# Layer 2: the first row's norm for the mixer, made and turned inside the FFN's steps of the second row

## The chip, the cores and the metric

The kernel runs on one core of a Trainium2 chip. Its time is the device time of one execution in microseconds. Of several executions the median counts.

## The reference, cut to what matters

The network has four layers on a float32 activation `x` of 2 rows (batch) x 512 tokens x 256 features. Every layer is a half-weighted FFN, a mixer and the same FFN again, each on a norm of `x` without weights:

```
def _layernorm(x, axis=-1, eps=1e-05):
    m = jnp.mean(x, axis=axis, keepdims=True)
    v = jnp.var(x, axis=axis, keepdims=True)
    return (x - m) / jnp.sqrt(v + eps)
...
    x = x + 0.5 * _L2_ffn_ref(_layernorm(x, axis=-1), L2_ffn_wg, L2_ffn_W, L2_ffn_b)
    x = x + _L2_attn_ref(_layernorm(x, axis=-1), L2_attn_W_in, ...)
    x = x + 0.5 * _L2_ffn_ref(_layernorm(x, axis=-1), L2_ffn_wg, L2_ffn_W, L2_ffn_b)
```

Layer 2's FFN is a routed one with 8 experts of 256 x 256. A token's logits go through a softmax, the best expert is taken, and its output plus bias is weighted by its probability. Layer 2's mixer is a state-space model with 8 heads of 64, a state of 128, a causal convolution of 4 taps, and a gate. Its input product is

```
        zxbcdt = u @ W_in
        z = zxbcdt[..., :D_INNER]
        xBC = zxbcdt[..., D_INNER:D_INNER + CONV_DIM]
        dt = zxbcdt[..., D_INNER + CONV_DIM:]
        dt = jax.nn.softplus(dt + dt_bias)
```

where `u` is the normed `x`. Every token of `u` needs only its own token of `x`. The mixer works along a row, and the two rows don't meet in it.

## The kernel before, in words

`x` stays on the chip for the whole program, as 8 chunks of 128 tokens (one token a partition). Chunks 0 to 3 are the first batch row, 4 to 7 the second. TensorE (PE) multiplies over partitions, so a normed chunk (tokens on partitions) has to be turned before it is multiplied by a weight. PE does that by a product with an identity (`transpose`), and ACT or DVE copies the result out of PSUM.

**Layer 2's FFN** (`l2_ffn`) goes through the chunks in steps. The step of chunk c computes its experts, two experts a product (`experts`, product at L1622, its two additions into `x` on DVE at L1627), turns the next chunk n = c + 1 (`turn`, L1590, copy at L1592), routes it (`route`, L1600 to L1614), and adds the biases of chunk c (`bias_turn` L1633, `bias` L1642 and L1643). The statistics of later chunks (`measure`, which calls `scale`: bn_stats and aggregate on DVE at L191 and L192, two operations on POOL at L200 and L201) run ahead. `centre` (L205) makes the normed chunk. All chunks of a row are final in `x` once their own step is over.

**Layer 2's mixer** (`mamba`, with `few` true, as it has one group of 8 heads) begins with `layernorm_T`. It makes a tile `xT` for the turned norm of both rows and gives out the steps by which a row gets there: `measure` (statistics of four chunks on DVE, L215 and L216; one pair of POOL operations for all four, L224 and L225), `norm` (four L230), `turn` (four transposes into a PSUM bank at L184, a copy by `evac` at L130 or L132). `row(0)` does all of these for row 0 at once. Then `decay_sums(0)` multiplies the row by the dt columns (`pd`, L1762) and goes on to softplus and the decays (L1765 to L1816); `conv_b` and `conv_c` multiply by the B and C columns (`pp`, L1823), scale on ACT (L1826), and add three taps on DVE (L1830). Row 1's statistics, norm and turns are placed among these steps. The decays are written to HBM and read back by DMA (L1801, L1924, L1927), and then the chunks of the row are worked on.

`warm` (L164) multiplies constants by constants into a PSUM tile that nobody reads. In front of the mixer `few` gives 4 of them.

**What sets the order.** The program is written as one stream; a planner then orders each engine's instructions by their dependencies and its own estimates of durations. `in_order` pins the order as written: in the FFN for PE alone, in the mixer's opening for PE, ACT and DVE, and in its steps for POOL too. What is not pinned, as DVE, ACT and POOL in the FFN, may be moved ahead or back. Engines run their instructions strictly in that order. A PSUM pool that opens on banks of a closed one waits for the closed one's last readers. `f2m`, the FFN's PSUM pool, has all 8 banks; the mixer's `psM` has 3 in rotation. The weights are fetched early: `wb` (B, C and dt columns) far ahead and `wx` (`fetch_wx`, L1876) on SP's queue before the FFN begins.

Layer 2's FFN is built twice, before and after the mixer; layer 3 follows with its own FFN and a larger mixer of the same function.

Of the kernel before, what the change touches and what calls it, by code (L numbers as in the profile page):

```python
# [10 lines left out]
F32 = mybir.dt.float32  # L11
# [7 lines left out]
P = 128  # L19
B, S, D = 2, 512, 256  # L20
T = B * S
NC = T // P
CB = S // P
KD = D // P
# [59 lines left out]
class Net:  # L84
# [143 lines left out]
    def layernorm(self, pool, xn, b, mv, rstd):  # L228
# [8 lines left out]
            )  # L237
        return xn

    def layernorm_T(self, es, psum):  # L240


        xT = es.enter_context(self.tc.tile_pool(name="xT", bufs=1)).tile([P, KD, T], F32, name="xT")
        p = es.enter_context(self.tc.tile_pool(name="ln", bufs=1))

        made = {}

        def measure(b):
            made[b] = self.scales(p, b)

        def norm(b):
            made[b] = self.layernorm(p, p.tile([P, CB, D], F32, tag="xn", name="xn"), b, *made[b])

        def turn(b, k):
            self.transpose_tokens(made[b], xT, psum, b, k)

        def row(b):
            if b in self.pending:
                by_chunks(b)
                return  # L260
            measure(b)
            norm(b)
            for k in range(KD):
                turn(b, k)

        def by_chunks(b):

            xn = p.tile([P, CB, D], F32, tag="xn", name="xn")
            ps = [psum.tile([P, S], F32, tag="mm", name="ps_tr") for _ in range(KD)]
            ms = {}  # L270
            for cc in range(CB + 1):
                if cc < CB:
                    self.settle(b, cc + 1)
                    ms[cc] = self.scale(p, b * CB + cc, b * CB + cc)
                if cc > 0:
                    j = cc - 1
                    self.centre(xn[:, j, :], b * CB + j, *ms[j])
                    if j < CB - 1:
                        self.warm(psum, 1)
                    for k in range(KD):  # L280
                        self.nc.tensor.transpose(
                            ps[k][:, j * P : (j + 1) * P], xn[:, j, k * P : (k + 1) * P], self.ident
                        )
            for k in range(KD):
                self.evac(xT[:, k, b * S : (b + 1) * S], ps[k])

        return xT, row, measure, norm, turn

    def rms(self, pool, out, h, w):
# [1249 lines left out]
    @contextmanager  # L1539
    def l2_weights(self):  # L1540

        nc, tc, a = self.nc, self.tc, self.a
        E = 8
        pre = "L2_ffn_"
        with tc.tile_pool(name="f2keep", bufs=1) as keep:
            self.w8T = keep.tile([P, KD, E, D], F32, name="w8T")
            self.b8 = keep.tile([E, D], F32, name="b8")
            self.wg8 = keep.tile([P, KD, E], F32, name="wg8")
            nc.sync.dma_start(self.wg8, a[pre + "wg"].rearrange("(k p) e -> p k e", p=P))
            nc.sync.dma_start(self.b8, a[pre + "b"])  # L1550
            with tc.tile_pool(name="f2pm", bufs=4, space=PSUM) as psM:
                for e0 in range(0, E, 4):
                    wn = self.w("w8")[:, : 4 * KD * D].rearrange("p (e c d) -> p e c d", e=4, c=KD)
                    for e in range(4):
                        nc.sync.dma_start(wn[:, e], a[pre + "W"][e0 + e].rearrange("(c p) d -> p c d", p=P))
                    for k in range(KD):
                        for e2 in range(0, 4, 2):
                            ps = psM.tile([P, 2, KD, P], F32, tag="mm", name="ps_w8")
                            for e in range(2):
                                for c in range(KD):  # L1560
                                    nc.tensor.transpose(
                                        ps[:, e, c, :], wn[:, e2 + e, c, k * P : (k + 1) * P], self.ident
                                    )
                            self.evac(
                                self.w8T[:, k, e0 + e2 : e0 + e2 + 2, :].rearrange("p e d -> p (e d)"),
                                ps.rearrange("p e c d -> p (e c d)"),
                            )
            yield

    def l2_ffn(self):  # L1570


        nc, tc = self.nc, self.tc
        E = 8
        with ExitStack() as es:
            sb = es.enter_context(tc.tile_pool(name="f2", bufs=3))
            st = es.enter_context(tc.tile_pool(name="f2s", bufs=1))
            psM = es.enter_context(tc.tile_pool(name="f2m", bufs=8, space=PSUM))
            ms, xts, ws, wTs = {}, {}, {}, {}

            def measure(c):
                ms[c] = self.scale(st, c, c)
# [54 lines left out]
            def bias(c):  # L1637
                if c < 0:
                    return
                xc = self.x[:, c, :]  # L1640
                pb = psM.tile([P, D], F32, tag="mm", name="pb")
                nc.tensor.matmul(pb, wTs[c], self.b8, start=True, stop=True)  # L1642
                nc.vector.tensor_tensor(xc, xc, pb, ALU.add)  # L1643

            tail = {}
            for c in range(-1, NC):
                n = c + 1
                if n == 0:
                    measure(0)
                    measure(1)  # L1650
                if n + 1 < NC and n:
                    measure(n + 1)
                with self.in_order(tail, ("PE",)):
                    experts(c, 0)
                    turn(n)
                    bias_turn(c)
                    experts(c, 1)
                    route(n)
                    experts(c, 2)
                    bias(c)  # L1660
                    experts(c, 3)


    mix = {}
# [43 lines left out]
    def mamba(self, pre, win, wout, nh):  # L1708
# [4 lines left out]
        nc, tc, a = self.nc, self.tc, self.a  # L1713
# [7 lines left out]
        few = NG == 1  # L1721
        wname, win, wout = win, a[pre + win], a[pre + wout]
        with ExitStack() as es:
            psM = es.enter_context(tc.tile_pool(name=pre + "m", bufs=3, space=PSUM))
            xT, row, measure, norm, turn = self.layernorm_T(es, psM)
# [366 lines left out]
            later = {}  # L2092
            tail = {}
            with self.in_order(tail, ("PE", "Activation", "DVE")):
                self.warm(psM, 4 if few else 18)
                row(0)
                fetch_wx(*order[0])
                d0, d1 = decay_sums(0), decay_sums(1)
                next(d0)
                b_taps, b_silu = conv_b(0)  # L2100
                c_taps, c_silu = conv_c(0)
                next(d0)
                unit(0)
                fetch_wx(*order[1])
                x = [prep_front(us[0], 0)]
                if few:
                    measure(1)
                b_taps()
                next(d0)
                next(d0)  # L2110
                if few:
                    norm(1)
                c_taps()
                next(d0)
                x[0][0]()
                if few:
                    turn(1, 0)
                    turn(1, 1)
                else:
                    self.settle(1)  # L2120
                x.append(prep_front(us[0], 1))
                next(d0)
                next(d0)
                next(d0, None)
                x[1][0]()
                for i in range(3):
                    chunk(i)
                b_silu()
                c_silu()
                products(0)  # L2130
                x[0][1]()
                x[1][1]()
                x.append(prep_front(us[0], 2))
                prep_back(us[0], 0)
                x[2][0]()
                x[2][1]()
                prep_back(us[0], 1)
                x.append(prep_front(us[0], 3))
                exponents(ks[0])
                x[3][0]()  # L2140
                x[3][1]()
                prep_back(us[0], 2)
                exponents(ks[1])
                if few:
                    next(d1)
                raised(ks[0])
                if few:
                    next(d1)
                    next(d1)
                back = (us[0], NM - 1)  # L2150
                if few:
                    later = {0: [d1.__next__, d1.__next__, d1.__next__], 1: [d1.__next__, lambda: next(d1, None)]}
                else:
                    parts = [lambda: measure(1), None, lambda: norm(1), lambda: turn(1, 0), lambda: turn(1, 1)]
                    parts += [d1.__next__] * 7 + [lambda: next(d1, None)]
                    later = {i: [f] for i, f in enumerate(parts) if f}


            for s in range(NS):
                n, cc = steps[s]  # L2160
# [118 lines left out]
```

## Time and profile before

| | us |
|---|---|
| median of 3 runs | 1943.05 (1939.87 to 1947.71) |
| the profiled execution | 2031.53 |
| its span, first to last instruction | 2029.7 |
| layer 2's first FFN (889 to 957) | 68 |
| from there to 978, the mixer's opening up to its decays | 21 |
| rest of the mixer (978 to 1091) | 113 |
| layer 2's second FFN (to 1163) | 72 |

The profiled execution is one, and slower than those of the median, so differences are taken within it, and the sum is made against its own time. In rows of the timeline the columns are start, duration, engine, line, operation, output and inputs, shape and count. Behind them, in square brackets, stands how long the engine had been idle and who ended that.

### The profile page before, as it was taken

To read this page: it belongs to the slowest core of one execution; us is meant where nothing else is said; L and a number is where in the kernel's file an instruction comes from. 1 tells how busy PE (TensorE), PEld (TensorE's weight loads), DVE (VectorE), ACT (ScalarE), POOL (GpSimd) and SP (SyncE) were. 2 spreads that over 40 slices of the span, in tenths; PEclk is the share of its full clock that TensorE was granted. 3 is DMA by queue.
4 is the path that set the end of the run, shared out by engine and by line. 5 is a ranking of instruction groups with operands and counts; after the bars stand their busy time and mean duration, and the time that the engine had idled before them with its cause. 6 is when DMAs were issued, how large, how long until landed. Compare 5 with 4: busy or idle time off the path is not lost. (4 is left out here: it accounts for less than half of the span.)

```text
span 2029.7 us, 30414 instructions
## 1 busy us (share of the span) xinstructions
PE 1801.1 (89%) x10914; PEld 1285.4 (63%) x10914; DVE 1148.8 (57%) x2747; ACT 806.3 (40%) x1404; POOL 916.5 (45%) x915
## 2 busy tenths in 40 slices
PE   6888889999888887899788998889999899999985
PEld 4566666566666664554565466557777677777664
DVE  4522238426232357666577653478777777777633
ACT  1122215411122215420563012278777677877111
POOL 3366646530666440110033125135667456767263
PEclk8999999999998998999899998899999999999998
DMA  8145551041444360000221012344454444443132
GB/s 310 58 158 156 160 196 65 6 152 37 149 151 151 108 216 1 1 22 0 94 97 31 0 58 88 108 148 156 151 166 146 135 156 156 163 151 125 44 99 93
DMA packets 117444, 226.54 MB, mean 112 GB/s; under 512 B 22382, under 2 KB 68828, under 8 KB 117014
## 3 DMA queue, kind: packets, MB, share of 16 engines
q1 hardware_dynamic: 88134, 170.17, 25.6%
q0 software_dynamic: 20608, 48.45, 7.4%
q10 hardware_dynamic: 8528, 5.72, 0.9%
q8 instruction: 95, 1.56, 0.3%
q14 instruction: 79, 0.65, 0.1%
HBM read 195.59 MB, written 41.81 MB: 117 GB/s over the span
## 5 line engine op out<-in xcount | busy, mean ns | idle before, releaser
L538 POOL DMA_INDIRECT xe<-table,sl_get x176 | 179.9, 1022 | 230.4 <-DVE sl_get L514 145.9
L596 POOL DMA_INDIRECT rows<-ye,sl_put x176 | 176.7, 1004 | 133.6 <-DVE ye L130 43.1
L566 PE MATMUL ps_gu<-we,xeT 128*128 128x352 f32 x704 | 233.8, 475 | 0.0
L591 PE MATMUL ps_ye<-we,hT 88*128 88x256 f32 x704 | 182.2, 402 | 44.6 <-issue 23.2
L591 PEld LDWEIGHTS ps_ye<-we,hT 88*128 88x128 f32 x704 | 137.1, 198 | 90.1 <-issue 30.3
L1830 DVE SCALAR_TENSOR_TENSOR xc<-pp,L_attn_cols,xc 128x511 f32<-128x511 f32 (+2 forms) x216 | 161.4, 747 | 28.2 <-ACT xc L1826 23.0
L571 DVE SCALAR_TENSOR_TENSOR he<-se,xe,ps_gu 128x176 f32<-128x176 f32 x176 | 68.3, 396 | 192.6 <-ACT se L570 108.0
L566 PEld LDWEIGHTS ps_gu<-we,xeT 128*128 128x128 f32 x704 | 132.3, 200 | 59.5 <-issue 7.3
L1961 PE MATMUL pz<-xT,wt 128*128 128x128 f32 x1152 | 143.6, 278 | 12.3 <-ACT xt L1910 6.2
L1937 DVE SCALAR_TENSOR_TENSOR lm<-lm,jb,top 128x128 f32<-128x128 f32 x576 | 153.6, 340 | 0.0
L1961 PEld LDWEIGHTS pz<-xT,wt 128*128 128x128 f32 x1152 | 136.2, 193 | 17.6 <-issue 9.2
L2046 PE MATMUL yacc<-wt,y 128*128 128x256 f32 x576 | 143.0, 391 | 2.5 <-POOL y L2016 2.2
L1823 PE MATMUL pp<-xT,wx 128*128 128x512 f32 x288 | 140.8, 612 | 4.6 <-issue 1.2
L570 ACT ACTIVATE se<-ps_gu 128x176 f32<-128x176 f32 x176 | 54.1, 317 | 224.8 <-PE ps_gu L566 139.3
L2016 POOL TENSOR_TENSOR y<-y,sg 128x512 f32<-128x512 f32 x72 | 91.7, 1274 | 102.7 <-DVE y L2015 101.5
L1954 POOL TENSOR_TENSOR ce<-ce,CT 128x1024 f32<-128x1024 f32 x54 | 127.9, 2369 | 0.0
L1622 PE MATMUL ps_y<-w8T,xT 128*128 128x512 f32 x256 | 122.1, 611 | 0.0
L2046 PEld LDWEIGHTS yacc<-wt,y 128*128 128x128 f32 x576 | 103.8, 189 | 25.4 <-issue 10.3
L1989 PE MATMUL py<-lm,xt 128*64 128x128 f32 x1152 | 108.6, 282 | 11.9 <-DVE lm L1946 3.9
L1946 DVE TENSOR_TENSOR lm<-lm,M 128x1024 f32<-128x1024 f32 x72 | 87.1, 1215 | 48.0 <-ACT lm L1942 45.4
L164 PE MATMUL warm<-cst 128*128 128x256 f32 x348 | 97.8, 422 | 16.6 <-PEq L708 8.8
L2027 POOL TENSOR_TENSOR sqs<-sqs,sq 128x512 f32<-128x512 f32 x56 | 71.3, 1274 | 90.2 <-ACT sq L2026 90.2
(403 smaller groups left out, 3507.3 us busy)
## 6 DMA issues: line engine op xcount, KB each, us to landing
lm<-rows SPq DMA_DIRECT2D x72, 512.0 KB
ce<-rows SPq DMA_DIRECT2D x54, 512.0 KB
rows<-zero POOLq DMA_DIRECT2D x16, 768.0 KB
y<-rows SPq DMA_DIRECT2D x16, 768.0 KB
we<-in_L_ffn_w_gate_dram SPq DMA_DIRECT2D x64, 176.0 KB
we<-in_L_ffn_w_up_dram SPq DMA_DIRECT2D x64, 176.0 KB
we<-in_L_ffn_w_down_dram SPq DMA_DIRECT2D x64, 176.0 KB
we<-in_L_ffn_w_dram SPq DMA_DIRECT2D x48, 176.0 KB
```

The costliest lines, as they stand in the source:

```text
L538: nc.gpsimd.indirect_dma_start(xe[:, i, :], None, table, bass.IndirectOffsetOnAxis(get[:, e * per + j : e * per + j + 1], 0), bounds_check ...
L566: nc.tensor.matmul(pg, xeT[:, k, i * P : (i + 1) * P], wgu[:, :, k], start=(k == 0), stop=(k == KD - 1))
L591: nc.tensor.matmul(py[:, i, :], hT[:, q, i * P : (i + 1) * P], wd[:, q, :], start=(q == 0), stop=(q == 1))
L596: put_rows = nc.gpsimd.indirect_dma_start(rows, bass.IndirectOffsetOnAxis(put[:, e * per + j : e * per + j + 1], 0), y[:, i, :], None, bou ...
L1622: nc.tensor.matmul(ps, xT[:, k, :], self.w8T[:, k, 2 * e2 : 2 * e2 + 2, :], start=(k == 0), stop=(k == KD - 1))
L1823: nc.tensor.matmul(pp, wv[:, k, :], xT[:, k, b * S : (b + 1) * S], start=(k == 0), stop=(k == KD - 1))
L1830: nc.vector.scalar_tensor_tensor(out[:, 3 - w :], pp[:, : S - 3 + w], cw[:, m, w : w + 1], out[:, 3 - w :], ALU.mult, ALU.add)
L1937: nc.vector.scalar_tensor_tensor(k["lm"][:, h, :], k["lm"][:, h, :], jb[:, k["c"], n : n + 1], top, ALU.add, ALU.min)
L1954: nc.gpsimd.tensor_tensor(k["ce"], k["ce"], ct, ALU.mult)
L1961: nc.tensor.matmul(pz[:, m, :], u["wz"][:, kk, m * P : (m + 1) * P], xT[:, kk, c * P : (c + 1) * P], start=(kk == 0), stop=(kk == KD - 1),)
L1989: nc.tensor.matmul(py[i * HP : (i + 1) * HP, m, :], w[:, h * HP : (h + 1) * HP], v[:, h, :], start=(m == 0 and n == 0), stop=(n == len(src ...
L2046: nc.tensor.matmul(yacc[cc // 2][:, cc % 2, :], k["y"][:, m, :], u["wo"][:, m, :], start=(u["g"] == 0 and m == 0 and cc % 2 == 0), stop=(u ...
```

## The change

A tile `into` (named `nxT`) of the shape of the mixer's `xT` is made once, with layer 2's weights, and lives from there to the layer's end. In the first FFN of the layer (the second finds none) two functions come in. `next_measure` makes the statistics and scale of a chunk of row 0 as it is after its FFN step. `next_turn` centres it with these, turns it by two transposes into one PSUM tile, and copies it by ACT into `into`. They are written into the steps c = 3 to 6 and 4 to 7: chunk c - 4 is turned between `bias` and the last pair of experts. `layernorm_T` takes that tile as its `xT`, and `row(0)` then returns at once. In front of this mixer there are no products of constants any more; layer 3's mixer keeps its 18.

```diff
+    turned = None
     def layernorm_T(self, es, psum):
-        xT = es.enter_context(self.tc.tile_pool(name="xT", bufs=1)).tile([P, KD, T], F32, name="xT")
+        xT, self.turned = self.turned, None
+        early = xT is not None
+        if not early:
+            xT = es.enter_context(self.tc.tile_pool(name="xT", bufs=1)).tile([P, KD, T], F32, name="xT")
...
         def row(b):
+            if b == 0 and early:
+                return
...
             self.wg8 = keep.tile([P, KD, E], F32, name="wg8")
+            self.into = keep.tile([P, KD, T], F32, name="nxT")
...
-            ms, xts, ws, wTs = {}, {}, {}, {}
+            ms, xts, ws, wTs, nms = {}, {}, {}, {}, {}
+            into, self.into = self.into, None
+            self.turned = into
+
+            def next_measure(c):
+                if into is not None and 0 <= c < CB:
+                    nms[c] = self.scale(st, f"n{c}", c)
+
+            def next_turn(c):
+                if c not in nms:
+                    return
+                xn = self.centre(sb.tile([P, D], F32, tag="nxn", name="nxn"), c, *nms.pop(c))
+                pt = psM.tile([P, KD, P], F32, tag="mm", name="pt_nx")
+                for k in range(KD):
+                    nc.tensor.transpose(pt[:, k, :], xn[:, k * P : (k + 1) * P], self.ident)
+                nc.scalar.copy(into[:, :, c * P : (c + 1) * P], pt)
...
                     route(n)
                     experts(c, 2)
                     bias(c)
+                    next_turn(c - 4)
                     experts(c, 3)
+                    next_measure(c - 3)
...
             with self.in_order(tail, ("PE", "Activation", "DVE")):
-                self.warm(psM, 4 if few else 18)
+                if not few:
+                    self.warm(psM, 18)
                 row(0)
```

## The prediction

> **What bounds the kernel now.** I read three views: the page for the whole program, the busy time by stage for layer 2, and the timeline between its first FFN and its mixer. The page says that TensorE (PE) is the busiest engine.
>
> ```profile
> PE 1801.1 (89%) x10914; PEld 1285.4 (63%) x10914; DVE 1148.8 (57%) x2747; ACT 806.3 (40%) x1404; POOL 916.5 (45%) x915
> ```
>
> A share over the span does not price a change in one place. The stages do (columns: window, its length, busy us and instructions of PE, PEld, DVE, ACT and POOL, the granted PE clock, DMA):
>
> ```profile
> 889.00:957.00 68.00, 67.47 (x197) 31.02 (x196) 42.17 (x139) 5.54 (x23) 0.61 (x2) 1.00 0.04 14
> 957.00:978.00 21.00, 17.72 (x54) 10.82 (x55) 10.83 (x37) 4.75 (x10) 2.55 (x4) 0.76 0.00 0
> ```
>
> In the FFN PE has no gap (67.47 of 68 us) while DVE works 42.17 us, ACT 5.54 and POOL 0.61: these three have room, PE has none. In the mixer's first 21 us the clock is 0.76 and PE waits. The timeline shows for what:
>
> ```profile
> 954.49 1.98 PE L1622 MATMUL ps_y<-w8T,xT 128*128 128x512 f32 x4
> 957.66 1.97 PE L164 MATMUL warm<-cst 128*128 128x256 f32 x8 [1.19 <-DVE x L1627]
> 961.51 1.38 DVE L230 TENSOR_SCALAR xn<-x,ln_mv,ln_rstd 128x256 f32<-128x256 f32 x4 [1.59 <-POOL ln_rstd L225]
> 961.98 1.87 PE L184 MATMUL ps_tr<-cst,xn 128*128 128x128 f32 x8 [2.35 <-DVE xn L230]
> 964.06 3.75 PE L1762 MATMUL pd<-wb,xT 128*128 128x8 f32 x16 [0.21 <-DVE xT L130]
> 967.66 6.67 PE L1823 MATMUL pp<-xT,wb 128*128 128x512 f32 x8
> 974.16 1.88 PE L1823 MATMUL pp<-xT,wx 128*128 128x512 f32 x4
> 974.36 0.69 ACT L1826 ACTIVATE CT<-pp,L_attn_cols 128x512 f32<-128x512 f32 x1 [2.22 <-PE pp L1823]
> 975.07 1.28 ACT L1773 ACT_TABLE_LOAD   x1
> 976.36 0.23 ACT L1773 ACTIVATE dA<-dt 128x32 f32<-128x32 f32 x1
> 976.62 0.19 DVE L1775 SCALAR_TENSOR_TENSOR dt<-dt,dt 128x32 f32<-128x32 f32 x1 [2.13 <-ACT dA L1773]
> ```
>
> FFN, then a norm on DVE and POOL, then transposes, then `pd`: a chain with one engine at work at a time. The two matrices it then multiplies by are no part of it: `wb` was asked for at 740.3 and `wx` at 887.2, and DMA is at 0.00 here. After it, eight products (`pp`, 967.66 to 974.3) run 0.83 us apart where the next four run 0.43 apart (from 974.16, the next group at 975.88): the half clock. ACT takes its turn after the second `pp`, and L1775 waits for ACT. I use the start of L1775 as the mark of the mixer's beginning; everything behind it (decay sums, rows to HBM and back, unit 0) hangs on it in a fixed order and moves with it.
>
> **The change, part by part.** The order of the built program's instructions, before against after, is the other source here.
>
> *1. Norm and turns leave the gap.* Four bn_stats/aggregate pairs, two POOL operations, four L230, eight transposes, two copies and the four constant products go. `pd` becomes the first user of the mixer's PSUM pool and inherits the wait of the product it replaces, for the last DVE addition into x (the same instruction by its semaphore count). So it starts where `warm` did, 957.66, and not 964.06: 6.40 us. Were that wait not there it could follow the FFN at 956.5, 1.2 us better; that is the bound on one side.
>
> *2. The clock.* At full clock 16 `pd` take some 1.8 us (16 x 0.11, from four `pl` products of the same 8 columns in 0.4) and two `pp` pairs 8 x 0.43 = 3.44: together 5.2 us, where the rows above show 964.06 to 974.3, 10.2. That would be 5.0 us more, 11.4 in all. Whether the clock stays up is the point to weigh, since four products that kept PE busy are gone. [...]
>
> ```profile
> 977.10:980.50 3.40, 1.71 (x12) 1.00 0.00 0
> 980.50:983.90 3.40, 1.63 (x11) 1.00 0.08 17
> 983.90:987.30 3.40, 3.40 (x6) 0.50 0.82 271
> 1001.00:1004.40 3.40, 2.20 (x16) 1.00 0.00 0
> 1004.40:1007.80 3.40, 3.40 (x9) 0.50 0.00 0
> ```
>
> With 1.63 us busy the next window ran at half; with 1.71 it did not. And 1001 to 1004.4 lost its clock with 2.20 us busy, mostly the second row's `pd`: 8 columns a product hardly count. In the changed kernel 1.2 us of wait and 1.8 of `pd` make 3 us of low activity. [...] By the row: 11.4 less 1.9 on average = 9.5. I take the row. Keep 11.4 (none lost) and 8.0 (two).
>
> DVE must keep up: `pd` ends near 959.5, the dt steps and row 1's four statistics take until 962.7 (3.2 us after `pd`, as in the rows of before: 967.8 to 971), three taps of 2.31 us end at 965.0; ACT's chain (second `pp` near 962.9, then 0.69 + 1.28 + 0.23 and hand-overs) ends at 965.2. So ACT still sets L1775, barely.
>
> *3. What the FFN takes on.* PE: eight transposes, two per step in steps 4 to 7. A pair took 0.22 us (`pt` at 941.76, the next instruction at 941.98); PE is full, so 4 x 0.22 = +0.9, up to 1.6 with seams. DVE: per chunk 0.4 + 0.1 for the statistics and 0.4 for L205; a step of 8.46 us has 5.2 to 5.4 DVE busy, so 6.1 to 6.3, hidden. POOL: 0.22 + 0.57 per chunk on an engine idle for 70 us. ACT: 0.37 per copy, 0.7 busy in a step. PE would wait only if a centred chunk were late: the order has the statistics of chunk 0 behind step 0 and the first three L205 in DVE's steps 1 to 3, one or more steps ahead of PE's use in 4 to 6; the fourth stands in step 4, behind the release of its buffer by the first transposes, and is used in 7. No DMA is moved; SP's order is unchanged.
>
> *4. What the planner moved elsewhere.* At the mixer's end DVE's order differs:
>
> ```profile
> 1083.85 0.42 DVE L191 BATCH_NORM_STATS2 ln_st<-x 128x6 f32<-128x256 f32 x1
> 1084.19 0.67 DVE L2015 TENSOR_TENSOR y<-xc,py 128x512 f32<-128x512 f32 x1
> 1085.01 1.27 POOL L2016 TENSOR_TENSOR y<-y,sg 128x512 f32<-128x512 f32 x1 [0.64 <-DVE y L2015]
> 1086.97 1.04 DVE L2037 TENSOR_REDUCE sqm<-sqs 128x128 f32<-128x512 f32 x1 [0.55 <-ACT sqs L2023]
> 1089.44 0.18 DVE L157 RECIPROCAL rs<-rs 128x4 f32<-128x4 f32 x1 [1.43 <-ACT rs L156]
> ```
>
> Before, the next FFN's first norms (L191 from 1080.72) stood ahead of the last L2015; now they stand behind both last L2037 and ahead of L157. L2015 can go at 1082.6, when `py` ends, so L2037 ends 1.6 us earlier, at 1086.4. But then the norms run, each L205 waiting for POOL: from the first L191 to the last of them took until 4.2 us later before (1080.72, third scale ready at 1084.36, then L205 and an aggregate). L157 comes at 1090.6 and not 1089.44: +1.2, and the four x updates, PSUM's release and the second FFN wait for it. At best L157 would follow ACT at 1087.9, a gain of 1.5; that needs the norms hidden, and in DVE's order they are not. [...] In layer 3's first FFN two small DVE operations leave the stretch before L230's second pair, and a copy waits: -0.3.
>
> *Sum:* -9.5 + 0.9 + 1.2 + 0.4 - 0.3 = -7.3 us. The profiled execution took 2031.53 us (span 2029.7); the sum gives 2024.2 there. The runs' median is 1943.05, 88 us lower; layer 2's PE stretches have no part of that gap that I can name, so I carry the 7.3 over unscaled: 1935.8 us, or -0.38%. A measurement of this kernel tells about 0.5% (9.7 us) from no change; its three runs spread over 7.8.
>
> **The rivals.** *More is won* (26%): the clock holds or the mixer's end costs nothing. -11.4 + 0.9 + 0.1 = -10.4, 1932.6. [...] Against: the 1001 row and DVE's order. *It hardly matters* (13%): something I take to move with L1775 does not, most likely the rows' way to HBM and back (written at 981.71) or the clock, down for two windows; 4 to 6 us are given back, -2, 1941. Against: that transfer is asked for by `cr`, itself in the chain. *Slower* (8%): PE, in order, waits at the four new turns in a full FFN. If L205 stood behind the bias addition of its own step (947.29 + 0.42, then 0.4), its transposes would start near 948.2 and not 946.7, and with DVE's extra 0.9 us of work about 2.4 us late: 4 x 2.4 = 9.6 of wait, -7.3 + 9.6 = +2.3, 1945. It decides from 1.8 us a step. The order of DVE, three of four well ahead, speaks against it. That the change does nothing is excluded: the order shows the eight transposes moved.
>
> **How the numbers follow.** My forecast has 53%. Of it, with the spread of the runs, about 5 of 53 fall below -9.7 us; of the first rival 20 of 26. Faster by over 0.5%: 25%; slower by over 0.5% needs +9.7 us, the far end of the last rival: 4%; within: 71%. The range: low from -11.4 - 1.2 and a run's spread, 1928.5; high from the second rival with the third's beginning and that spread, 1944.
>
> **What would show it.** Right: `pd` about 1.2 us behind the last `ps_y`; L1775 9 to 11 us behind the end of the last FFN product, before 20.1 (976.62 less 956.5); a clock of 0.5 for one window during `pp`; FFN steps 4 to 7 each about 0.22 us longer; L157 about 8 us after the last `py`, before 6.9. Wrong: PE idle ahead of the new transposes; `pd` waiting for ACT's copies; the stretch from L1775 to the end of the last `py` (1082.6) longer than the 106 us of before by more than 2.

## The result, and the profile after

The changed kernel takes 1936.94 us (median of 19 runs, 1930.91 to 1947.13). The kernel before, run beside it, takes 1943.36 (19 runs, 1936.2 to 1949.41). The ratio is 0.9975 with a 95% interval of 0.9963 to 0.9986: about 4.9 us less (2.7 to 7.2), where the forecast was 7.3 less. That is faster, and within 0.5%. (The two medians lie 6.4 us apart. The ratio is the figure that has an interval, so savings of whole runs are told by it here.)

The profiled execution of the changed kernel has a span of 1936.0 us; that of before had 2029.7. The 94 us between them are not the change: 64 of them have passed before layer 2's first FFN starts (first `ps_y` at 889.2 before, at 824.9 after), and some 26 more lie behind layer 3's router. So I compare lengths inside layer 2.

| stretch, us | before | after | difference |
|---|---|---|---|
| first FFN, first `ps_y` to the turn in step 4 | 35.66 | 37.16 | +1.50 |
| from there to the end of its last `ps_y` | 31.64 | 32.33 | +0.69 |
| to the first `pd` | 7.59 | 1.30 | -6.29 |
| to the decays (L1775, now L1801) | 12.57 | 7.76 | -4.81 |
| to the end of the mixer's last `py` | 105.96 | 106.13 | +0.17 |
| to the reciprocal L157 | 6.86 | 8.02 | +1.16 |
| to the second FFN's first `ps_y` | 3.40 | 4.02 | +0.62 |
| second FFN, to the end of its last `ps_y` | 69.00 | 69.42 | +0.42 |
| to the copy of layer 3's router logits | 13.69 | 16.60 | +2.91 |
| sum | 286.36 | 282.74 | -3.62 |

Line numbers of the mixer are 26 higher after the change. The page's line of busy time, which says little here, as before:

```profile
PE 1759.9 (91%) x10906; PEld 1267.4 (65%) x10906; DVE 1150.2 (59%) x2746; ACT 810.5 (42%) x1407; POOL 918.6 (47%) x921
```

The windows by stage, FFN and opening (columns as before: window, length, PE, PEld, DVE, ACT, POOL, clock, DMA):

```profile
824.90:894.50 69.60, 69.53 (x203) 32.15 (x203) 45.47 (x151) 7.04 (x27) 3.50 (x9) 0.98 0.03 13
894.50:903.50 9.00, 7.52 (x30) 4.34 (x31) 5.90 (x19) 3.37 (x7) 1.28 (x2) 1.00 0.00 0
```

The FFN still has no gap on PE with the added work (69.53 of 69.60). Its clock is 0.98: one window at half clock (824.56 to 827.97, at 0.50) fell on its first microseconds. That is the +1.50 of the table's first row. It belongs to the execution and not to the change: seven of the nine other kernels below have 35.66 in that row, and two have 37.0 to 37.2, one of them without any of the added FFN work. (In the traces of before and after the granted clock is 1.0 or 0.5. The stretches at half clock are 3.41, 6.83 or 10.24 us long, but for the last, which runs over the program's end, and in each trace they start whole multiples of 3.41 us apart. A "window" is one such 3.41 us.) The opening is 9.06 us instead of 20.15, at full clock. Its timeline:

```profile
892.55 1.88 PE L1646 MATMUL ps_y<-w8T,xT 128*128 128x512 f32 x4
...
895.73 1.92 PE L1788 MATMUL pd<-wb,nxT 128*128 128x8 f32 x16 [1.30 <-DVE x L1651]
...
897.51 3.68 PE L1849 MATMUL pp<-nxT,wb 128*128 128x512 f32 x8
...
901.02 1.88 PE L1849 MATMUL pp<-nxT,wx 128*128 128x512 f32 x4
...
901.23 0.69 ACT L1852 ACTIVATE CT<-pp,L_attn_cols 128x512 f32<-128x512 f32 x1 [0.97 <-PE pp L1849]
...
901.93 1.28 ACT L1799 ACT_TABLE_LOAD   x1
...
903.49 0.19 DVE L1801 SCALAR_TENSOR_TENSOR dt<-dt,dt 128x32 f32<-128x32 f32 x1 [0.48 <-ACT dA L1799]
```

`pd` follows the FFN and waits, as forecast, for the FFN's last addition on DVE. The eight `pp` take 3.68 us where they took 6.67, and the chain to L1801 runs through ACT. One step of the FFN with an added turn:

```profile
867.02 0.44 PE L1602 MATMUL pt_nx<-cst,nxn 128*128 128x128 f32 x2
867.30 3.60 PE L1646 MATMUL ps_y<-w8T,xT 128*128 128x512 f32 x8
867.50 0.37 ACT L1603 COPY nxT<-pt_nx 128x256 f32<-128x256 f32 x1 [1.77 <-PE pt_nx L1602]
```

PE has no wait ahead of this turn, nor ahead of the other three. At the mixer's end:

```profile
1009.66 0.69 DVE L2041 TENSOR_TENSOR y<-xc,py 128x512 f32<-128x512 f32 x1 [2.58 <-PE py L2015]
...
1012.48 1.04 DVE L2063 TENSOR_REDUCE sqm<-sqs 128x128 f32<-128x512 f32 x1 [1.18 <-ACT sqs L2049]
...
1014.66 0.26 ACT L156 ACTIVATE rs<-pr,eps 128x4 f32<-128x4 f32 x1 [0.91 <-PE pr L2085]
...
1017.22 0.41 DVE L205 TENSOR_SCALAR xn<-x,ln_mv,ln_rs 128x256 f32<-128x256 f32 x1
...
1017.63 0.14 DVE L157 RECIPROCAL rs<-rs 128x4 f32<-128x4 f32 x1
```

ACT has the square root ready at 1014.9, and DVE comes to L157 at 1017.63, behind the next FFN's norms. The costliest surprise is at layer 3's start. First before, then after (SPq rows are DMA issues by SP):

```profile
1091.45 0.29 SPq L338 DMA_DIRECT2D router<-in_L_ffn_gate_w_dram  x1
...
1162.98 0.26 PE L342 MATMUL ps_rt<-cst,router 8*128 8x8 f32 x2 [1.15 <-issue]
1163.17 1.99 PE L164 MATMUL warm<-cst 128*128 128x256 f32 x8
```

```profile
1089.09 1.98 PE L1646 MATMUL ps_y<-w8T,xT 128*128 128x512 f32 x4
...
1092.27 0.29 SPq L345 DMA_DIRECT2D router<-in_L_ffn_gate_w_dram  x1
...
1093.80 0.26 PE L349 MATMUL ps_rt<-cst,router 8*128 8x8 f32 x2 [2.73 <-DMA router<-in_L_ffn_gate_w_dram]
1093.98 3.59 PE L164 MATMUL warm<-cst 128*128 128x256 f32 x8
```

Before, the router's weights were asked for at the mixer's end, 71.5 us ahead of their use. Now the request comes 1.2 us behind the second FFN's last product, and PE waits 2.73 us for it, where it was idle for 1.15 before. The eight products of constants behind it then run at half clock (3.59 us for 1.99; the clock is 0.50 from 1094.21 to 1097.62). So the +2.91 are 1.6 us of wait and 1.6 of clock, less 0.2 behind them. What SP waited for ahead of this request, before and after (waiter, what ended the wait, us in total, times, longest):

```profile
SPq L338 <- DVE x L2064: 1.7, 1, 1.7
SPq L345 <- DVE x L1651: 77.0, 1, 77.0
```

L2064 is an addition into `x` at the mixer's end; L1651 is the second FFN's last one.

### The profile page after: what moved, and what is told of

Its sections match the earlier page's. It is cut to its first block, busy times and chain, and to the rows that moved or that the text cites. A ratio compares the mean times of both kernels' runs of the same rounds, so it can differ in the third digit from the quotient of the medians.

```text
span 1936.0 us, 30401 instructions
## 1 busy us (share of the span) xinstructions
PE 1759.9 (91%) x10906; PEld 1267.4 (65%) x10906; DVE 1150.2 (59%) x2746; ACT 810.5 (42%) x1407; POOL 918.6 (47%) x921
## 5 line engine op out<-in xcount | busy, mean ns | idle before, releaser
L573 PE MATMUL ps_gu<-we,xeT 128*128 128x352 f32 x704 | 224.6, 460 | 0.0
L598 PE MATMUL ps_ye<-we,hT 88*128 88x256 f32 x704 | 168.1, 379 | 2.9 <-ACT ye L132 1.7
L573 PEld LDWEIGHTS ps_gu<-we,xeT 128*128 128x128 f32 x704 | 126.3, 190 | 55.4 <-DVE xeT L130 1.3
L598 PEld LDWEIGHTS ps_ye<-we,hT 88*128 88x128 f32 x704 | 133.1, 190 | 36.7 <-ACT ye L132 3.6
L1987 PE MATMUL pz<-xT,wt 128*128 128x128 f32 x1024 | 128.3, 279 | 7.7 <-ACT xt L1936 4.7
L1987 PEld LDWEIGHTS pz<-xT,wt 128*128 128x128 f32 x1024 | 121.7, 194 | 10.8 <-ACT xt L1936 5.7
L1849 PE MATMUL pp<-xT,wx 128*128 128x512 f32 x256 | 121.6, 598 | 1.4 <-DVE jb L1835 0.6
L2072 PEld LDWEIGHTS yacc<-wt,y 128*128 128x128 f32 x576 | 103.8, 189 | 23.9 <-issue 10.1
```

Of the source, the lines that this page charges most:

```text
L573: nc.tensor.matmul(pg, xeT[:, k, i * P : (i + 1) * P], wgu[:, :, k], start=(k == 0), stop=(k == KD - 1))
L598: nc.tensor.matmul(py[:, i, :], hT[:, q, i * P : (i + 1) * P], wd[:, q, :], start=(q == 0), stop=(q == 1))
L1849: nc.tensor.matmul(pp, wv[:, k, :], xT[:, k, b * S : (b + 1) * S], start=(k == 0), stop=(k == KD - 1))
L1987: nc.tensor.matmul(pz[:, m, :], u["wz"][:, kk, m * P : (m + 1) * P], xT[:, kk, c * P : (c + 1) * P], start=(kk == 0), stop=(kk == KD - 1),)
L2072: nc.tensor.matmul(yacc[cc // 2][:, cc % 2, :], k["y"][:, m, :], u["wo"][:, m, :], start=(u["g"] == 0 and m == 0 and cc % 2 == 0), stop=(u ...
```

## The experiments

Times of the kernel before beside the runs are 1943 to 1944 us, but for the run of the tile's place alone. Stretches of a kernel are read from its one profile. The nearest question was the +2.91 us.

**The tile given back at the mixer's end.** In the built programs `nxT` lies 8 KB per partition among the layer's weights, and the pools opened after it lie 8 KB higher: the second FFN's turned chunks then share addresses with layer 3's `router`, and its load has to wait for their last reader. The traces show no addresses. They do show the wait: the load waits for a semaphore of PE that it does not wait for before. What ends the wait, though, is DVE's last addition (1092.13), 1.0 us behind PE's last signal. Here `nxT` has a pool of its own that closes with the mixer.

```diff
-            self.into = keep.tile([P, KD, T], F32, name="nxT")
+            self.freed = ExitStack()
+            self.into = self.freed.enter_context(tc.tile_pool(name="nx", bufs=1)).tile([P, KD, T], F32, name="nxT")
...
-        if not early:
+        if early:
+            es.push(self.freed)
+        else:
             xT = es.enter_context(self.tc.tile_pool(name="xT", bufs=1)).tile([P, KD, T], F32, name="xT")
```

> The changed kernel, with the 8 KB tile nxT in a pool of its own that closes with the mixer, so that the second FFN of layer 2 lies where it lay before. Theory: two of the costs behind the mixer are the tile's address, not the change itself. The router weights of layer 3 are asked for ahead of the second FFN again (70 us before their use, not after its end), from the end of the FFN's last expert product to the router's logits in SBUF it takes 13.7 us and not 16.6, and the norms stand ahead of the mixer's last gating again, so L157 comes 6.9 us after the last py and not 8.0. In all 4 us below the changed kernel: 1933, ratio to the kernel before about 0.995. Rival: the 2.9 us at layer 3 are the clock, cold in that place by chance in one profile; then the stretch stays at 14 to 17 us and the time like the changed kernel's, 1937.

Measured: 1937.68 us median of 11, ratio 0.9958 (0.9942 to 0.9975), so about 8.2 us less than before. The median is not the 1933 expected, and it lies 5.7 us below that of before, no farther than the changed kernel's 6.4: the totals don't tell these two apart. The stretches do. From the second FFN to the router logits 13.69 us, L157 6.82 us behind the last `py`:

```profile
1016.39 0.18 DVE L157 RECIPROCAL rs<-rs 128x4 f32<-128x4 f32 x1 [1.43 <-ACT rs L156]
...
1018.40 0.29 SPq L347 DMA_DIRECT2D router<-in_L_ffn_gate_w_dram  x1
```

The load is early again (its product comes some 71 us later), and L157 waits for ACT, not for norms. Both losses go with the tile's place, while opening (9.06) and FFN (35.66 and 32.33) stay as in the changed kernel.

**The tile's place alone.** The reverse test: the kernel before, with `nxT` among the layer's weights as the mixer's `xT`, and nothing else of the change.

```diff
 # against the changed kernel
-                if into is not None and 0 <= c < CB:
+                if False:
...
-            if b == 0 and early:
-                return
...
-                if not few:
-                    self.warm(psM, 18)
+                self.warm(psM, 4 if few else 18)
```

> The kernel before with one thing of the change: the 8 KB tile of the turned norms is set aside from the FFN's weights to the layer's end, and the mixer uses it in place of its own; both rows are still normed and turned in the mixer, and the four products of constants stay. Theory (the tile's place alone makes layer 3's router load wait, and gives the 1.16 us at the mixer's end): from the second FFN's last product to layer 3's router logits 16.6 us instead of 13.7, the reciprocal L157 8.0 us behind the last py instead of 6.86, the opening up to L1801 at 20.15 us or up to two clock windows less, the first FFN at 35.66 and 31.64; so about 4 us slower than before, ratio 1.002. Rival (the load waits because the changed FFN or the mixer runs in another order, and the tile's place is only a part of it): 13.7 us, or L157 at 6.9, and no slower than before.

Measured: ratio 1.0011 (0.9989 to 1.0034), on a chip where the kernel before takes 2047.61 us; the total alone decides nothing. The stretches decide: 16.68 us to the router logits, L157 8.06 behind the last `py`, the FFN at 35.66 and 31.64.

```profile
1100.58 0.14 DVE L157 RECIPROCAL rs<-rs 128x4 f32<-128x4 f32 x1
```

```profile
1175.46 0.29 SPq L343 DMA_DIRECT2D router<-in_L_ffn_gate_w_dram  x1
1177.04 0.20 PEld L347 LDWEIGHTS ps_rt<-cst,router 8*128 8x128 f32 x2 [3.61 <-POOL xe L658]
1177.07 0.26 PE L347 MATMUL ps_rt<-cst,router 8*128 8x8 f32 x2 [2.81 <-DMA router<-in_L_ffn_gate_w_dram]
```

Eight kilobytes that are kept, and none of the moved work, give +3.0 us at layer 3's start and +1.2 at the mixer's end. Of all eleven profiles only the two with the kept tile are off 13.7 us at layer 3's start, by 2.9 and 3.0. That the tile's place changes the order at the mixer's end is so shown from both sides; by what path stays open.

**The side work alone.** The FFN's added work is done and its result is not used (the tile's pool closes with the FFN); the mixer norms both rows itself, behind its four products of constants.

```diff
 # against the kernel before: next_measure, next_turn and the tile, and
+            if into is not None:
+                es0.push(self.freed)
...
+                    next_turn(c - 4)
...
+                    next_measure(c - 3)
```

> The FFN makes and turns the first row's norm as in the changed kernel, but nobody uses it: the mixer makes its own as before, with the four constant products. The time of the opening is then not that of the change; only the FFN's steps are read. Theory: PE takes on its eight transposes and nothing else; from the turn in step 4 to the end of the FFN 32.3 us (31.64 in the kernel before, 32.33 in the changed one), 20 us from there to L1775 as before, the whole 0.7 above before. Rival: PE waits for the centred chunks: over 34 us.

Measured: 32.33 us in the FFN's second half, +0.69, as expected; the work that moved in is paid on PE alone. One run, 1942.61 us, is too little for a total. The opening, which is that of before, took 16.67 us here, with one window at half clock where the profile of before had three (963.45 to 973.69).

**The constants alone.** The kernel before without the four products of constants.

```diff
-                self.warm(psM, 4 if few else 18)
+                if not few:
+                    self.warm(psM, 18)
```

> The kernel before without its four constant products in front of layer 2's mixer, nothing else. Theory: they stand beside the norm's chain and only feed the clock, which drops anyway in the opening; from the FFN's end to L1775 20 us, give or take one cold window of 1.7. Rival: they hold the clock up for the first transposes; then L1775 is 2 to 4 us later than in the kernel before.

Measured: 19.84 us to the decays, within the 16.7 to 20.15 that the opening with them took. So no gain is seen in taking the constants out while the norm is still in the gap. (1948.9 us, one run.)

**The constants kept** in the version with the given-back tile.

```diff
-                if not few:
-                    self.warm(psM, 18)
+                self.warm(psM, 4 if few else 18)
```

> The version with the given-back tile, and the four products of constants kept in front of the mixer. They are not in the reference's work and the output does not use them. Theory (the constants are cheap when nothing of the norm is left behind them, and they keep the clock window full): from the FFN's last product to the decay product 1.30 + 1.95 = 3.25 us, and to the decay sums' first update (L1801 in the changed kernel) 11.0 us, 1.95 above the 9.06 us of two runs of the changed kind; no 0.5-clock window before that update. Rival (the products matter for the clock): the runs without them would be those that are slow, so this one would stand at or below 9.1 us. Second rival (they lie in the 1.3 us in which the decay product waits for DVE, and cost only the rest): 9.06 + 0.65 = 9.7 us.

```profile
893.21 1.97 PE L164 MATMUL warm<-cst 128*128 128x256 f32 x8 [1.19 <-DVE x L1654]
895.01 1.85 PE L1791 MATMUL pd<-wb,nxT 128*128 128x8 f32 x16
```

Measured: `pd` 2.99 us behind the FFN, the decays 10.67 behind it, no window at half clock before them: near the theory's 11.0. The constants now inherit the wait for DVE, and `pd` stands behind them: they cost 1.6 us against the 9.06 of an opening that holds its clock anyway, and nothing against 10.75, which an opening that lost a window took (next experiment). Which is better on average stays open. Beside the 18.8 us that the opening of before takes on average over three profiles, the moved norm alone, with the constants kept, is worth some 8 us. (1936.31 us, one run.)

**The second FFN's norms behind L157.** The version with the given-back tile, and the subtraction L205 of the second FFN's first chunks bound behind the mixer's last update of `x`.

```diff
-                xn = self.centre(sb.tile([P, D], F32, tag="xn", name="xn"), c, *ms.pop(c))
+                tail = {"DVE": self.behind} if self.behind is not None else {}
+                with self.in_order(tail, ("DVE",)):
+                    xn = self.centre(sb.tile([P, D], F32, tag="xn", name="xn"), c, *ms.pop(c))
...
             add_row(B - 1)
+            self.behind = self.nc.cur_bb.bb.instructions[-1] if few else None
```

> As the kernel with the tile given back, and besides L205 of the second FFN's first chunks is bound behind the last x update of the mixer. Theory: L157 was late since L205 waits for POOL in front of it. It comes 5.4 us after the last py (6.9 before, 8.0 in the changed kernel), the first turn of the second FFN 0.4 us later behind it than before, some 1 us won in all: 1932. Rival: L157 waits for the last products and ACT's square root only, and the norms were hidden: no change against the kernel with the tile given back.

Measured: ratio 0.9966 (0.9952 to 0.9981), L157 6.93 us behind the last `py` (1009.38): the expectation missed.

```profile
1009.42 0.69 DVE L2046 TENSOR_TENSOR y<-xc,py 128x512 f32<-128x512 f32 x1 [0.15 <-PE py L2020]
...
1011.34 0.57 POOL L201 TENSOR_TENSOR ln_rs<-ln_rs,mhalf 128x1 f32<-128x1 f32 x1
1011.88 1.26 POOL L2047 TENSOR_TENSOR y<-y,sg 128x512 f32<-128x512 f32 x1
```

DVE is on time, 0.04 us behind `py`. But on POOL the norms' pairs L200 and L201 stand in front of the gate's product, which then starts at 1011.88, 1.8 us after its input (1010.11). I had moved the queue of one engine and left that of the other.

**POOL too.** The same, with L200 and L201 bound behind POOL's last gating.

```diff
-                ms[c] = self.scale(st, c, c)
+                tail = {"Pool": self.gated} if self.behind is not None else {}
+                with self.in_order(tail, ("Pool",)):
+                    ms[c] = self.scale(st, c, c)
...
                 nc.gpsimd.tensor_tensor(y, y, k["sg"], ALU.mult)
+                self.gated = self.nc.cur_bb.bb.instructions[-1]
```

> The version with the given-back tile, with the second FFN's first norms put behind the mixer's last updates on both engines: DVE's subtraction (as in the run where the norms stood behind the last reciprocal) and POOL's pairs ahead of it. Theory (at the mixer's end POOL's norms stand in front of its last gating, which the last chunk's x update waits for): POOL's gating comes at once, the reciprocal L157 5.3 to 5.5 us behind the last py instead of 6.8 to 6.9, the second FFN's first turn is 0.3 to 0.4 us later behind it, so about 1.1 us less than the version with the given-back tile; ratio to the kernel before 0.995. Rival (the chain behind the last py is set by ACT's reads and the statistics, not by POOL or DVE): 6.8 us as before, and nothing is gained. Second rival (the norms, now behind the chain, are late themselves): L157 early, but the second FFN's start 1.5 us or more later behind it, and the sum is unchanged or worse.

```profile
1011.37 0.69 DVE L2048 TENSOR_TENSOR y<-xc,py 128x512 f32<-128x512 f32 x1 [0.15 <-PE py L2022]
...
1012.23 1.27 POOL L2049 TENSOR_TENSOR y<-y,sg 128x512 f32<-128x512 f32 x1 [5.01 <-DVE y L2048]
...
1016.67 0.18 DVE L157 RECIPROCAL rs<-rs 128x4 f32<-128x4 f32 x1 [1.44 <-ACT rs L156]
```

Measured: L157 5.34 us behind the last `py` (1011.33), the second FFN's turn 2.34 behind that instead of 2.02: 1.16 us less than with the tile given back, as expected in this place. In this profile most of it is lost again: the second FFN's first turn takes 0.66 us (0.41 with the tile given back; 0.66 in the changed kernel, where the clock is 0.50), and from it to the FFN's end it is 71.35 us, where 70.36 were taken with the tile given back. The total, 1935.97 us (median of 22), ratio 0.9963 (0.9947 to 0.9979), doesn't tell it from 0.9958.

**Another PSUM bank for `pd`.** The version with the given-back tile; the FFN has five banks in turn instead of eight, and the mixer's decay pool is opened first, on a bank that the FFN doesn't use.

```diff
-            psM = es.enter_context(tc.tile_pool(name="f2m", bufs=8, space=PSUM))
+            psM = es.enter_context(tc.tile_pool(name="f2m", bufs=5, space=PSUM))
...
+            if few:
+                psA = es.enter_context(tc.tile_pool(name=pre + "a", bufs=1, space=PSUM))
...
-            psA = es.enter_context(tc.tile_pool(name=pre + "a", bufs=1, space=PSUM))
+            if not few:
+                psA = es.enter_context(tc.tile_pool(name=pre + "a", bufs=1, space=PSUM))
```

> The version with the given-back tile, but the decay product's PSUM bank is one that the FFN does not use (the FFN has 5 banks in turn instead of 8). Theory (the 1.30 us ahead of the decay product are a wait for the FFN's last addition on DVE, passed on by the PSUM pool): the decay product starts 0.1 to 0.3 us behind the FFN's last product, the decay sums' first update comes about 8.0 us behind it instead of 9.06; the FFN's stretches stay at 35.66 and 32.33 us, the second FFN's at 68.7. Rival (PE waits at that place for another thing, the weights' load or the turned tile): still 1.3 us. Second rival (five banks are too few): the FFN's two stretches grow by 0.3 us or more each, and the gain is gone.

Measured: `pd` follows the FFN without a gap (it starts 0.16 us ahead of the last product's end, which the profile models), and the decays come 7.52 behind the FFN instead of 9.06; the FFN stays at 35.66 and 32.34. Nothing but the PSUM pools differs, so the 1.30 us were a wait that they handed on, and five banks are enough. (1934.31 us, one run.) The second FFN took 70.23 instead of the 68.7 expected, with two half-clock windows at its start; the next kernel, with the same five banks, took 68.99.

**Both** (POOL and DVE bound, and the bank): the diffs of the last three together.

> Both of the last two edits in one kernel. Theory: their gains add, 1.1 us at the mixer's start and 1.1 us at its end, so about 2.2 us below the version with the given-back tile: 1933 us or a little less beside a kernel before of 1943, ratio 0.994 to 0.995. Rival (one of the two does not do what it says): 1.1 us or nothing, which the stretch from the FFN's last product to the decay product and the one from the last py to the second FFN's first product tell apart.

Measured: 1928.06 us median of 7 beside 1944.05, ratio 0.992 (0.9893 to 0.9948): the best of all, and more than the 0.994 to 0.995 expected. `pd` follows the FFN without a gap, the decays come 7.52 behind it, L157 5.34 behind the last `py`.

```profile
898.15 1.88 PE L1653 MATMUL ps_y<-w8T,xT 128*128 128x512 f32 x4
...
899.87 1.85 PE L1798 MATMUL pd<-wb,nxT 128*128 128x8 f32 x16
900.08 0.48 DVE L1658 SCALAR_TENSOR_TENSOR x<-ps_y,w,x 128x256 f32<-128x256 f32 x1 [1.18 <-PE ps_y L1653]
```

`pd` now starts ahead of DVE's last addition, which it used to wait for. The ratio says 15.6 us; the stretches account for about 11.8 (opening 18.8 to 7.5, with the mean of the three openings of before; L157 1.5; the added turns and the later second turn give back 1.0), which lies inside the interval (10.1 to 20.8). The rest is not explained. The mixer from the decays to its last `py` took 104.05 us in this profile and 105.17 with the bank alone, where the other nine have 105.9 to 108.3; whether the bank does that or the clock stays open.

## Why the prediction was right, and where not

The time forecast was 1935.8 us and the time is 1936.94. One step of the sum had the wrong sign and missed by 3.2 us, which is more than the whole forecast missed by. So the close number is in part luck: by the ratio the gain is 4.9 us and not 7.3, and the measured terms below add up to less still.

*Norm and turns leave the gap, -6.40:* right. `pd` waits 1.30 us for DVE (forecast 1.2), and the opening's start moved by 6.29. The bound "it could follow the FFN ... 1.2 us better" is what the other bank showed, with 1.54 us in the decays.

*The clock:* forecast 9.5 for both steps together, 11.4 if the clock holds. In the pair of profiles it is 11.1, and the half-clock window forecast during `pp` isn't there. Over all profiles it is less. Four openings of the changed kind with that 1.30 us wait took 9.06, 9.06, 10.75 and 10.75; three of the kind before took 20.15, 19.56 and 16.67. Means 9.9 and 18.8: 8.9 us won. So the profile of before was at the dear end of its own opening, which I had taken as fixed; that, and not the new opening, made the term a little too large. No run shows the 1.9 us on average that the forecast took off the 11.4: of these four openings two kept their clock and two lost one window, 1.69 us each (10.75 against 9.06) and 0.85 on average, with PE waiting 1.30 us in all four. Where the clock was kept, the window that covers the FFN's end reaches 1.8 and 2.0 us behind that end, and where it was lost 3.0 and 3.1 (last section).

*What the FFN takes on, +0.9:* +0.69, by the side work alone too. A turn costs 0.17 us and not 0.22, and no turn waited: the late L205 of the rival "Slower" didn't occur.

*The planner's changes elsewhere:* L157 stands 8.02 us behind the last `py`, the +1.2 of the forecast to 0.04. The order forecast is there, norms ahead of L157. But it is no part of the moved work: the tile's place alone gives it, and the tile given back takes it away. The second FFN's start at half clock (the +0.4 of the sum): no run shows that term by itself. From its first turn to its end it took 70.38 us before and 71.46 after, +1.08, with one window at half clock at its start before (1093.15 to 1096.56) and two after (1019.12 to 1025.94); the other kernels lie between -0.05 and +1.7 there.

*The failed step* is "In layer 3's first FFN two small DVE operations leave the stretch ...: -0.3", with "No DMA is moved; SP's order is unchanged." The order was unchanged indeed; what changed was what SP's load waits for. With a tile that lives to the layer's end, the load waits until the second FFN's last addition, and where it had 71.5 us of cover it has none: +2.91 instead of -0.3. What the step did name may have come, as the 0.2 us that the stretch is shorter behind the products of constants. I compared the order of the queue and not its waits, and gave the kept tile no cost because it has no instruction.

*The sum again,* with the measured terms: -8.9 + 0.7 + 1.2 + 2.9, and the forecast 0.4 for the second FFN's start, is -3.7, where the runs say -4.9 (-7.2 to -2.7). Without the two terms of the tile's place it is -7.8, where the kernel that gives the tile back has -8.2 by its ratio (-11.3 to -4.9).

*The rivals:* "More is won" has the opening of the two profiles (-11.1) and not the total. "It hardly matters" falls: from the decays to the rows' write it is 5.09 us as before (5.08), and to the last `py` 106.13 (105.96), so what hangs on the decays moved with them. One profile could hide a shift here, as the mixer's time at half clock differs (three windows there before, four after). Over all eleven it took 104.1 to 108.3 us, with a mean of 106.5 in the four that have the norm in the opening and 106.3 in the seven that don't.

## What to carry to other kernels

A tile that lives longer can cost through its place (here 3.0 us at layer 3's start and 1.2 at the mixer's end): look at what the pools opened after it now lie on, and compare the waits of early loads as well as their order. Give such a tile a pool that closes with its last reader. Where work is moved behind a critical chain, move it in the queue of every engine that it uses, or the wait goes to the one left out (1.8 us on POOL here). And take the cost of a stretch whose clock varies (16.67 to 20.15 us in the opening of before) from several executions, not from one.

## What was not expected of the hardware

In these profiles busy time alone doesn't say whether the clock is kept behind a window. Two windows in the same stretch of two kernels with the same opening, and the window behind each; the changed kernel first, then the kernel with DVE's norms behind L157:

```profile
892.82:896.24 3.42, 2.12 (x9) 0.92 (x7) 1.55 (x4) 0.51 (x2) 0.00 (x0) 1.00 0.00 0
896.24:899.65 3.41, 3.41 (x18) 2.30 (x18) 1.56 (x8) 0.31 (x2) 0.00 (x0) 1.00 0.00 0
```

```profile
890.40:893.81 3.41, 2.11 (x16) 1.72 (x16) 1.13 (x3) 0.21 (x1) 0.00 (x0) 0.99 0.00 0
893.81:897.22 3.41, 3.41 (x7) 1.74 (x7) 2.51 (x12) 0.23 (x1) 0.00 (x0) 0.51 0.00 0
```

PE is busy for 2.12 us in one and 2.11 in the other. In the first, 1.6 of them are products with 512 columns (the FFN ends at 894.43); in the second 0.4 (it ends at 890.82), and the rest are `pd` with 8. Only the second loses the clock behind it (0.51, where the first has 1.00). In the four profiles with this opening, which of the two happens goes with where the windows fall: the changed kernel's window ends 1.8 us behind the FFN, the other's 3.0. The other two kernels with this opening agree: with the tile given back the window ends 2.0 us behind the FFN, has 2.12 us busy and keeps the clock; with POOL bound too it ends 3.1 behind, has 2.11 busy and loses it.

The chip on which the tile's place was tried alone takes 2047.61 us for the kernel before, 104 more than the others. Layer 2's first FFN has the same length there (35.66 and 31.64), and 75 us more have passed when it starts (899.4 against 824.9). That profile shows 99 us at half clock in this part where the changed kernel's shows 48. At half speed the 51 us more cost at most some 25 us by my estimate, so most of the 75 has another cause, which stays open. The profile of before looks the same (FFN at 889.2, 89 us at half clock ahead of it), which may be why its span is so long.
